# Another table of rank corrections and other tiling weights in the list scheduler of an attention kernel with a second, adapter attention

## The chip, the cores and the metric

The kernel runs on one NeuronCore of a Trainium2 chip. One execution of the whole program is timed on the device, in microseconds; the time of a version is the median of its runs. Engines are named as the profile names them: PE is TensorE, PEld its loading of weights, DVE VectorE, ACT ScalarE, POOL GpSimd and SP the engine that issues most of the transfers.

## The reference, cut to what matters

`x` is (2, 2048, 640), the context (2, 128, 384); there are 8 heads of 80. In what follows S is 2048, the last T = 4 rows of the context are `ca`, the 124 ahead of them `enc`.

```python
query  = x @ Wq                                   # (2, 2048, 640)
hs     = mha(query, enc @ Wk, enc @ Wv)           # text attention, 124 keys
ca_q1  = einsum('btc,th->bch', ca, Wq_ca)         # (2, 384, 640): one row for each of the 384 features of ca
ca_q1  = ca_q1[:, linspace(0, 383, S).astype(int)]  # row s of the output uses one of these 384 rows
ca_hs1 = mha(ca_q1, x, x)                         # the adapter's first attention, over all 2048 rows of x
ca_hs2 = mha(ca_hs1 @ Wq, ca @ Wk_ca, ca @ Wv_ca) # its second one, over 4 keys
out    = (hs + ca_hs2) @ Wout + b_out + x
```

`mha(q, k, v)` splits the 640 columns into 8 heads, and is softmax(q k^T / sqrt(80)) v for each head. All is float32.

## The kernel before, in words

**Tiles.** The 2 x 2048 rows of x are cut into 8 blocks of 512 rows, written (batch, number), and into 16 units `m` of 256 rows, two tiles of 128 each.

**Queries.** `queries_fast` multiplies a block by Wq in a scheme of four "chains" of products on sums of halves of x and Wq: matmuls `pq`, weights 128x128, 256 columns each, inputs `xt` (x transposed), `xs` (differences of x) and `wq_sb`. A product collected in a PSUM bank is copied to `q` by ACT or DVE if it is the first of its part, and added by DVE otherwise. The fifth group of 128 columns goes by `plain`; its result leaves for device memory through ACT and DVE (`halves_away`) and comes back in another layout over `landing`, by four transfers on SP (`rest_back`), from which ACT copies the `rests`.

**Text attention of a unit.** `text_scores`: matmuls `sc`, in tiles of 64x128, for each of the two row tiles. `softmax`: DVE's maximum `m`, eight exponentials `p` on ACT with their sums, a reciprocal `r`, the normalization (by whichever of POOL, DVE and ACT is free first), then DVE's transpose into `eb`, of which there is one buffer, and a transfer of `eb` to `kept` in device memory. `probabilities` brings `kept` back as `pT` (two buffers) and calls `text_out_fast`: matmuls `ph` in tiles of 128x32 into `hs` (copied by ACT or DVE), then matmuls `po` with Wout or sums of it, 128x128, 320 columns each, in four chains; DVE adds every result to the unit's rows of x. These rows lie in eight buffers (`x_more` and `last_rows`), are loaded by `residual` through SP and stored when complete. The adapter's result for those rows is added to them by a gathering transfer on POOL.

**Adapter, one pass for each batch.** `yz_block` makes for each block the operands `yz` and `zop` of x times the adapter's weights, and through DVE (`zs`, `yt`) and device memory the rows `y_sb`. The first loop of `adapter` runs over 4 blocks, 3 column tiles and 2 halves: four matmuls `s` (32x128) into a buffer of four PSUM banks, `quad`, then DVE's maximum `mx` of all four. There is one `quad`, so each piece of `s` waits for the maximum of the piece before. After the 24 maxima comes the **hand-over**: DVE writes `mt`, PE turns it (`pm`), DVE adds it to `ca`, ACT and DVE make the operand `cop` of it. Then the second loop, 24 pieces for each of two halves `j`: matmuls `s` into `quad`, ACT's exponential `ea`, and matmuls `acc` (128x32) with `y_sb` by `contract`. `second` does the attention over four keys with the result. The pass of batch 1 begins while that of batch 0 ends:

```python
        if b + 1 < B:
            yield Fork(adapter(b + 1), 0)
```

**What sets the order.** None of this is written in the order in which it runs. Each of the functions above is a generator that yields steps `Do(engine, fn, ...)`, and a class `Desk` replays them while the program is built, with estimated durations (`matmul`, `transpose`, `__getattr__`, `dma`). In `run` it takes at each point the engine that can begin something first, and among the steps that could begin at that earliest time on that engine the one with the least sum of two numbers:

```python
                    t, op = min(
                        (x for x in found if x[0] <= t + 1e-9),
                        key=lambda x: self.order(x[1]) + self.change(x[1].mode),
                    )
```

`order` is the rank that the code gives to the task or the step (for instance 10 + 2n for the queries of block n, 30 + m for the output of unit m, 2 + 0.1n for the loads of x of block n), plus a correction for this one task: `begin` counts the tasks of each name as they are begun and looks the n-th of them up in the table `RANKS`. A task is one run of a generator, so "chain" 30 is the 31st chain to be begun, of the queries' or of the output's, and "softmax" 21 the 22nd row tile. A lower number goes first. `change` is a weight that is added only where the step is marked with a tiling of PE (`mode`) other than the present one: `LEAVE` if the present one is the whole array (128x128), `SWITCH` for going back to the whole array, `ANOTHER` between two others. Only `pq`, `sc`, `ph` and `po` are marked.

The times and tilings serve only to choose. What is built is a fixed list of instructions for each engine, in the order in which the steps were taken (line 208 of the profile is the one place where matmuls are issued, 218 transposes, 233 everything of DVE, ACT and POOL, 253 SP's transfers, 2107 POOL's gathers), and waits on data and buffers hold them together on the chip. Where a step may go to several engines, the replay also decides which one does it.

Of the kernel before, what the change touches and what calls it, by code (L numbers as in the profile page):

```python
# [14 lines left out]
P = 128  # L15
# [49 lines left out]
class Desk:  # L65
# [1 line left out]


    ENGINES = ("PE", "ACT", "DVE", "POOL", "SP", "NONE")
    WHOLE, SWITCH, LEAVE, ANOTHER = (P, P), 157.7, 5.4, 131.2  # L70
    START = {(P, P): 0.107, (64, P): 0.143, (P, 64): 0.107, (64, 32): 0.1, (P, 32): 0.03}
    DRAIN = {
        ((P, P), (32, P)): 0.136, ((P, P), (64, P)): 0.035, ((P, P), (P, 64)): 0.056, ((P, P), (P, 32)): 0.067,
# [9 lines left out]


    RANKS = {
        "adapter": {0: 3, 1: 5.5},
        "chain": {2: 9, 4: -18, 5: 11, 6: -3, 8: -1, 10: -8, 11: -0.6, 19: -3, 24: -3, 25: 8, 30: 11, 32: 8,
            34: -10, 35: -1, 36: -1.3, 39: 2, 41: 3.5, 42: 4, 45: 6, 48: -4, 49: -15, 52: -1, 53: 6, 58: 8,
            60: -6, 61: -6, 62: -9, 64: -1, 72: -3, 80: 2, 85: 3, 87: 7},
        "contract": {0: 5.5, 1: 6, 2: 6, 3: 8},  # L90
        "halves_away": {1: -13, 2: -2, 6: 7},
        "keys": {0: -11},
        "probabilities": {0: 6.1, 8: 9, 9: 6, 11: -7, 14: -3, 15: 4},
        "queries_fast": {0: 4, 4: -3},
        "rest_back": {1: 13, 4: 5, 9: 7, 10: 8},
        "second": {0: 6},
        "softmax": {0: 6, 2: -2, 4: -5, 8: 5, 10: 4, 11: -4, 14: -4, 16: 2, 17: 7, 21: 12, 22: 10, 25: 4},
        "sums_of_wq": {0: 9},
        "text_scores": {0: -3, 1: 9, 12: 5},
        "values_weights": {0: -17},  # L100
        "x_load": {1: 5.1, 4: 7, 5: 6},
        "y_rows": {2: 4, 3: 15, 5: -2},
        "yz_block": {2: 12, 3: -2, 6: 10, 7: 1.3},
    }

    def __init__(self, tc):
# [2265 lines left out]
```

## Time and profile before

| | |
|---|---|
| median of 3 runs | 588.07 us (587.85 to 589.9) |
| profiled execution, its own time | 588.11 us |
| its span in the trace | 586.4 us |
| granted clock of PE | full in all 40 slices |
| PE | 578.6 us busy, 99%, 4681 instructions |
| weight loads, PEld | 374.8 us, 64% |
| DVE | 392.0 us, 67% |
| ACT | 313.2 us, 53% |
| POOL | 141.7 us, 24% |
| moved by transfers | 112.27 MB, mean 191 GB/s |

The span is the time between the first and the last record of the trace; the execution's own time has something more around it. "Busy" for PE counts a matmul from its start to a modelled end, and matmuls overlap in the pipeline, so that PE's share hides short waits. DVE, ACT and POOL are counted by records with measured ends. A line of groups gives line, engine, operation, output and inputs with shapes, the count, then the busy time and the mean of one in ns, then the idle time ahead and what ended most of it. A line of the chain or of the timeline begins with the start and the duration in us. A line of waits names who waited, for whom, and the total, the count and the longest.

### The profile page before, as it was taken

Reading aid. Unit: us, or ns where it says so; the run is one execution under the profiler, and the core shown is the slowest. Engines: PE = TensorE matmul, PEld = TensorE weight load, DVE = VectorE, ACT = ScalarE, POOL = GpSimd, SP = SyncE. Lnnn points to the kernel's source line nnn. Section 1 sums busy time; section 2 is a strip of 40 time slices with the busy share of each in tenths; the row PEclk is TensorE's granted clock in tenths of the full one; section 3 lists DMA queues with packets and bytes.
Section 4 is the critical chain, followed back from the end, with each engine's and each line's share of the span. In section 5 each row is a group of like instructions: output and inputs, shape, how many; then the busy total and the mean of one; then the engine's idle time right before and its main releaser. Section 6 shows DMA issues by size and latency. Waiting matters only on the chain.

```text
span 586.4 us, 12250 instructions
## 1 busy us (share of the span) xinstructions
PE 578.6 (99%) x4681; PEld 374.8 (64%) x4681; DVE 392.0 (67%) x646; ACT 313.2 (53%) x881; POOL 141.7 (24%) x200
## 2 busy tenths in 40 slices
PE   9999999999999999999999999999999999999997
PEld 8786446676766566566576656655556566676675
DVE  2546899999999566356999999853255353544443
ACT  1413276686558789679847626368678612102200
POOL 9102112112205214010115225122041221322342
PEclk9999999999999999999999999999999999999999
DMA  8996876899566967324999959994658577699967
GB/s 254 231 215 116 204 105 180 173 212 182 148 198 149 219 144 193 114 75 155 246 264 260 235 150 206 295 265 122 154 124 248 128 198 201 142 261 267 264 162 195
DMA packets 153012, 112.27 MB, mean 191 GB/s; under 512 B 83701, under 2 KB 126581, under 8 KB 152954
## 3 DMA queue, kind: packets, MB, share of 16 engines
q1 hardware_dynamic: 147322, 100.80, 66.5%
q0 software_dynamic: 5632, 10.69, 10.5%
q8 instruction: 37, 0.61, 0.4%
q14 instruction: 21, 0.17, 0.1%
HBM read 71.23 MB, written 40.22 MB: 190 GB/s over the span
## 4 chain that ended last, share of the span: by engine, by line
PE 85%; DVE 9%; DMA 2%; issue 2%; ACT 2%; DVEq 0%
PE po L208 27%; PE pq L208 23%; PE acc L208 7%; PE ph L208 7%; PE sc L208 6%; PE s L208 6%; DVE mx L233 4%; PE pyz L208 2%; DVE eb L233 1%; PE pv L208 1%; PE pk L208 1%; DMA kept<-eb 1%; DMA zb<-z 1%; DVE m L233 1%; PE unread L208 1%
## 5 line engine op out<-in xcount | busy, mean ns | idle before, releaser
L233 DVE TENSOR_REDUCE mx<-s 128x4 f32<-128x2048 f32 x48 | 109.3, 2276 | 2.4 <-PE s L208 2.4
L233 ACT ACTIVATE ea<-s 128x2048 f32<-128x2048 f32 x48 | 91.0, 1895 | 30.8 <-PE s L208 30.6
L233 ACT ACTIVATE p<-sc,m 128x124 f32<-128x124 f32 x256 | 89.8, 383 | 7.5 <-DVE m L233 6.8
L208 PE MATMUL pq<-xt,wq_sb 128*128 128x256 f32 (+1 forms) x312 | 86.2, 416 | 0.1
L208 PE MATMUL po<-wout_sums,hs 128*128 128x320 f32 x256 | 78.9, 440 | 0.5 <-DVE x_more L233 0.5
L208 PE MATMUL po<-wout_sb,hs 128*128 128x320 f32 x248 | 76.6, 439 | 0.0
L233 DVE TENSOR_TENSOR x_more<-x_more,po 128x320 f32<-128x320 f32 x76 | 36.5, 484 | 52.3 <-PE po L208 51.8
L208 PEld LDWEIGHTS pq<-xt,wq_sb 128*128 128x128 f32 x312 | 56.8, 190 | 21.3 <-issue 13.7
L208 PEld LDWEIGHTS po<-wout_sums,hs 128*128 128x128 f32 x256 | 47.2, 190 | 23.6 <-issue 4.7
L208 PEld LDWEIGHTS po<-wout_sb,hs 128*128 128x128 f32 x248 | 45.6, 190 | 22.8 <-issue 4.2
L233 ACT ACTIVATION_READ_ACCUMULATOR p<-sc,m 128x1 f32 x256 | 57.9, 226 | 0.0
L2107 POOL DMA_INDIRECT x_more<-o,query x19 | 29.4, 1550 | 101.2 <-DVE x_more L233 86.5
L208 PE MATMUL acc<-ea,y_sb 128*32 128x384 f32 (+2 forms) x768 | 51.2, 385 | 0.0
L233 DVE TENSOR_REDUCE m<-sc 128x4 f32<-128x496 f32 x64 | 40.0, 662 | 11.2 <-PE sc L208 11.1
L233 DVE TENSOR_TENSOR last_rows<-last_rows,po 128x320 f32<-128x320 f32 x52 | 25.0, 485 | 31.6 <-PE po L208 31.2
L233 ACT COPY hs<-ph 128x512 f32<-128x512 f32 (+1 forms) x34 | 18.3, 545 | 51.7 <-PE ph L208 51.7
L208 PE MATMUL ph<-pT,vpad 128*32 128x256 f32 x768 | 45.0, 381 | 0.0
L233 ACT ACTIVATE p<-p,r 128x124 f32<-128x124 f32 x120 | 36.3, 387 | 10.9 <-DVE r L233 10.9
L233 POOL TENSOR_TENSOR p<-p,r 128x992 f32<-128x992 f32 x8 | 14.8, 1853 | 112.8 <-DVE r L233 112.8
L233 DVE STREAM_TRANSPOSE eb<-p 128x1024 f32<-128x1024 f32 x32 | 39.4, 1232 | 1.9 <-DMA kept<-eb 1.1
L208 PE MATMUL pq<-xt,wq 128*128 128x512 f32 (+1 forms) x90 | 40.1, 564 | 0.0
L208 PEld LDWEIGHTS sc<-kmain,q 64*128 64x128 f32 x512 | 31.5, 187 | 11.4 <-issue 6.1
(212 smaller groups left out, 814.7 us busy)
## 6 DMA issues: line engine op xcount, KB each, us to landing
kept<-eb SPq DMA_DIRECT2D x32, 512.0 KB, 4.4
pT<-kept SPq DMA_DIRECT2D x64, 256.0 KB, 6.7
landing<-away SPq DMA_DIRECT2D x60, 128.0 KB, 3.6
xi<-in_x_dram SPq DMA_DIRECT2D x56, 128.0 KB, 3.9
x_more<-in_x_dram SPq DMA_DIRECT2D x19, 320.0 KB, 6.6
out_dram<-x_more SPq DMA_DIRECT2D x18, 320.0 KB, 4.9
last_rows<-in_x_dram SPq DMA_DIRECT2D x13, 320.0 KB, 5.5
y<-yt SPq DMA_DIRECT2D x16, 256.0 KB, 3.5
```

Source lines behind the costliest of these rows:

```text
L208: self.pin(self.nc.tensor.matmul(out, lhsT, rhs, **kw))
L233: self.pin(getattr(engine, what)(*args, **kw))
L2107: desk.pin(nc.gpsimd.indirect_dma_start(out=t, out_offset=None, in_=o2_of[b], in_offset=bass.IndirectOffsetOnAxis(ap=query[:, st : st + 1] ...
```

## The change

Two things in `Desk` are replaced, and nothing else. The three weights of `change` become larger: 328.5 for 157.7 (`SWITCH`), 9.9 for 5.4 (`LEAVE`) and 185.7 for 131.2 (`ANOTHER`). And `RANKS`, the table of corrections for single tasks, is another one: tasks named in it go earlier or later in the replay than before. Every function that yields steps, every shape, buffer and estimated duration stays, and so do the numbers of matmuls and transfers; what differs in the program is the order of instructions on each engine, and for a few steps that more than one engine may do, the engine. The whole diff:

```diff
--- before.py
+++ after.py
@@ -67,7 +67,7 @@
 
 
     ENGINES = ("PE", "ACT", "DVE", "POOL", "SP", "NONE")
-    WHOLE, SWITCH, LEAVE, ANOTHER = (P, P), 157.7, 5.4, 131.2
+    WHOLE, SWITCH, LEAVE, ANOTHER = (P, P), 328.5, 9.9, 185.7
     START = {(P, P): 0.107, (64, P): 0.143, (P, 64): 0.107, (64, 32): 0.1, (P, 32): 0.03}
     DRAIN = {
         ((P, P), (32, P)): 0.136, ((P, P), (64, P)): 0.035, ((P, P), (P, 64)): 0.056, ((P, P), (P, 32)): 0.067,
@@ -83,24 +83,25 @@
 
 
     RANKS = {
-        "adapter": {0: 3, 1: 5.5},
-        "chain": {2: 9, 4: -18, 5: 11, 6: -3, 8: -1, 10: -8, 11: -0.6, 19: -3, 24: -3, 25: 8, 30: 11, 32: 8,
-            34: -10, 35: -1, 36: -1.3, 39: 2, 41: 3.5, 42: 4, 45: 6, 48: -4, 49: -15, 52: -1, 53: 6, 58: 8,
-            60: -6, 61: -6, 62: -9, 64: -1, 72: -3, 80: 2, 85: 3, 87: 7},
-        "contract": {0: 5.5, 1: 6, 2: 6, 3: 8},
-        "halves_away": {1: -13, 2: -2, 6: 7},
-        "keys": {0: -11},
-        "probabilities": {0: 6.1, 8: 9, 9: 6, 11: -7, 14: -3, 15: 4},
-        "queries_fast": {0: 4, 4: -3},
-        "rest_back": {1: 13, 4: 5, 9: 7, 10: 8},
-        "second": {0: 6},
-        "softmax": {0: 6, 2: -2, 4: -5, 8: 5, 10: 4, 11: -4, 14: -4, 16: 2, 17: 7, 21: 12, 22: 10, 25: 4},
-        "sums_of_wq": {0: 9},
-        "text_scores": {0: -3, 1: 9, 12: 5},
-        "values_weights": {0: -17},
-        "x_load": {1: 5.1, 4: 7, 5: 6},
-        "y_rows": {2: 4, 3: 15, 5: -2},
-        "yz_block": {2: 12, 3: -2, 6: 10, 7: 1.3},
+        "adapter": {0: 1, 1: 2},
+        "chain": {2: 8, 4: -11, 5: 7, 6: -2, 8: -11, 11: -4, 14: 11, 15: 16, 19: -14, 24: -4, 25: 3, 30: 3.1,
+            32: 4, 34: 10, 36: 2, 41: 0.5, 42: 1, 43: 0.5, 44: -10, 45: -10, 48: -8, 50: -5, 51: -5, 52: 7,
+            54: 10, 55: 10, 56: 10, 68: -4, 76: -3, 81: 2, 86: 2, 87: 3},
+        "contract": {0: 5, 1: 4.5, 2: 8, 3: 8},
+        "halves_away": {1: -4, 2: -2, 4: 4, 6: 6},
+        "keys": {0: -10},
+        "probabilities": {3: -8, 5: -4, 8: 12, 9: -3, 10: -2, 12: 6, 13: 6, 15: 7},
+        "queries_fast": {0: 5, 3: 4},
+        "rest_back": {1: 11, 4: 5, 7: 8, 9: 9, 10: 5, 14: 2},
+        "second": {0: 2.3},
+        "softmax": {0: 5, 2: -7, 3: 6.2, 4: -4, 7: -11, 8: 2, 10: -5, 12: -20, 14: -3, 17: 9, 20: -2, 21: 7,
+            22: 7, 25: -5, 29: 2, 30: 6},
+        "sums_of_wq": {0: 5.7},
+        "text_scores": {0: -8, 1: 3.4, 12: 9},
+        "values_weights": {0: -18},
+        "x_load": {1: 4.2, 4: 5},
+        "y_rows": {2: 2, 3: 6, 4: 4},
+        "yz_block": {2: 16, 5: 3.5, 6: 5},
     }
 
     def __init__(self, tc):
```

## Prediction

> **What bounds the kernel now.** I read the page first, then TensorE's waits, then the chain of work that ended last, then pieces of the timeline.
>
> ```profile
> span 586.4 us, 12250 instructions
> ...
> PE 578.6 (99%) x4681; PEld 374.8 (64%) x4681; DVE 392.0 (67%) x646; ACT 313.2 (53%) x881; POOL 141.7 (24%) x200
> ...
> DVE  2546899999999566356999999853255353544443
> ...
> PEclk9999999999999999999999999999999999999999
> ```
>
> TensorE (PE) works from end to end at full clock; VectorE (DVE) is full only in slices 6 to 13 and 20 to 25 of 14.66 us, about 73 to 190 and 279 to 366 us. The profiled execution took 588.11 us, 1.7 around its span, beside a median of 588.07: I sum against the former and carry the difference over unchanged.
>
> ```profile
> PE pm L218 <- ACT p L233: 0.7, 1, 0.7
> PE s L208 <- DVE mx L233: 0.6, 1, 0.6
> PE po L208 <- DVE x_more L233: 0.5, 1, 0.5
> ```
>
> These are the longest of TensorE's waits in the answer for 170 to 400 us (waiter, releaser; total, count, longest, us), and they look like nothing. But modelled ends hide short ones, so I compared starts with what the steps should take. The chain gives the steps:
>
> ```profile
> 1.12 3.78 PE unread L208 x16
> ...
> 7.19 8.65 PE pq L208 x40
> ...
> 197.95 1.86 PE acc L208 x32
> ...
> 203.24 1.00 PE acc L208 x16
> ...
> 553.47 29.28 PE po L208 x108
> ```
>
> A 256-column row steps by 8.65 / 40 = 0.216 us, a 320-column row by 29.28 / 108 = 0.271. A change of tiling costs something on top:
>
> ```profile
> 227.93 1.07 PE L208 MATMUL acc<-ea,y_sb 128*32 128x384 f32 x16
> 228.93 2.86 PE L208 MATMUL pq<-xt,wq_sb 128*128 128x256 f32 x12
> 231.72 0.56 PE L208 MATMUL s<-cop,zop 32*128 32x128 f32 x8
> ```
>
> From the start of pq to that of s are 2.79 us, and 12 rows are 2.59: leaving the whole array costs 0.20. Two acc pieces take 1.86, one 1.00, so a piece is 0.86 and leaving 128x32 costs 0.14. Summing columns and changes so over all 4681 rows from the first start (1.12), TensorE would end at 572.3 us; it ends at 553.47 + 29.28 = 582.7, after which the last addition and store take 3.7. So 10.3 us are lost in waits: by the starts, 3.5 before 105 us (the cold stretch and the first loads), 1.5 from 105 to 187, 0.8 to 265, 2.2 to 310, 0.4 to 363, 0.8 to 392 and 1.1 from there to the end. That list is all a new order has to win from, except for the changes of tiling themselves.
>
> **The change, part by part.** Only order moves: both programs hold the same 2803 matmuls, 441 transfers on SP and 64 on POOL. So I read the built orders.
>
> *Tiling weights.* 157.7 or 328.5 for going back to the whole array, 131.2 or 185.7 for going to a third tiling: each exceeds every difference of rank there is, so "stay in the tiling if anything is ready" holds before and after. Counted in the orders, stretches of one tiling go from 303 to 301: whole array 103 to 100, 128x32 63 to 64, the other kinds unchanged. That is 3 x 0.20 - 0.14 = 0.46 us less. [...]
>
> *Same order, same waits.* TensorE's order is the old one up to 152 us (but for one piece of pq at 105) and again from 252 to 310. The 3.5 and the 2.2 us stay; in the latter DVE is full with the maxima and its order is the old one but for which half of zop comes when.
>
> *First hand-over, 152 to 187 us.* The matmuls of the s loop wait for DVE's maximum of the piece before.
>
> ```profile
> L233 DVE TENSOR_REDUCE mx<-s 128x4 f32<-128x2048 f32 x48 | 109.3, 2276 | 2.4 <-PE s L208 2.4
> L233 ACT ACTIVATE ea<-s 128x2048 f32<-128x2048 f32 x48 | 91.0, 1895 | 30.8 <-PE s L208 30.6
> ...
> L233 DVE STREAM_TRANSPOSE eb<-p 128x1024 f32<-128x1024 f32 x32 | 39.4, 1232 | 1.9 <-DMA kept<-eb 1.1
> ```
>
> I step through DVE's new order by the trace's durations (less 0.08 each, by which DVE's rows overlap), from a maximum that stands where it stood:
>
> ```profile
> 155.85 2.28 DVE L233 TENSOR_REDUCE mx<-s 128x4 f32<-128x2048 f32 x1
> ...
> 173.62 2.28 DVE L233 TENSOR_REDUCE mx<-s 128x4 f32<-128x2048 f32 x1
> ```
>
> It ends at 158.1. An addition to q, one eb, a reciprocal and, newly ahead, three xt take 3.6: next maximum 161.7 to 164.0, and TensorE asks at 164.9. Then zs, q, yt and two m, 3.0: maximum 166.9 to 169.2, asked for at 168.9, so 0.3 us of waiting. Then zs, a reciprocal and eb: maximum 171.0 to 173.3, in time. Then q, yt, xt and two m: the last maximum ends at 178.6, and behind another eb mt comes at 180.5, 0.1 late for pm. TensorE's next pq want the banks that the two additions to mt free, 0.25 and 0.2 late, as an xt, two q, a difference of x and an m are queued ahead of them. Before, pm had to wait 0.7 us for a bank that ACT's exponentials held; now more pq stands ahead of pm, and that goes. With what is lost from 137 to 155 us as before, 1.3 replaces 1.5.
>
> *ACT's loop, 187 to 265 and from 385 on.* Each s2 waits for the exponential ea of the piece before, 1.9 us. Comparing, from each ea to the next, ACT's work with TensorE's, the places where ACT has more sum to 16.2 us before and 11.4 after; most are caught up from slack. I take 0.2 us off each of the two stretches.
>
> *Second hand-over, 363 to 392 us.* Before, it runs like this:
>
> ```profile
> 370.88 0.50 PE L208 MATMUL s<-zop,cop 32*128 32x512 f32 x4
> 376.46 0.52 PE L218 MATMUL pm<-ident,mt 128*128 128x128 f32 x3
> 378.40 0.55 PE L218 MATMUL pm<-ident,mt 128*128 128x128 f32 x3
> 385.57 0.50 PE L208 MATMUL s<-cop,zop 32*128 32x384 f32 x8
> ```
>
> ```profile
> 382.27 6.33 DMA kept<-eb
> 388.69 1.25 DVE eb L233
> 390.36 1.34 PE po L208 x4
> ```
>
> ```profile
> 379.67 0.55 DVE L233 TENSOR_TENSOR mt<-ca,pm 128x384 f32<-128x384 f32 x1
> ...
> 383.31 1.01 DVE L233 SCALAR_TENSOR_TENSOR cop<-cop,low_c,mt 128x768 fp32r<-128x768 f32 x1
> ```
>
> From the last s of one pass to the first of the next are 14.7 us; in between DVE takes the maximum, mt, two additions and cop. Shortly after, an eb waits 6.33 us for the store of the one before (there is one buffer), DVE's queue stands, and po waits 0.57 for an addition behind it. In the new order only 12.0 us of TensorE's work lie between the two s, but DVE's share there is shorter: 0.5 to the maximum's start, 2.2 for it, 1.2 for one eb, three additions, mt and pm 0.4 + 0.9, two additions to mt 0.55 each with others between, ACT's copy of cop some 0.9, cop 1.0. Queued in that order cop is done 10.1 us after the s, 1.9 before TensorE asks. The wait of eb for its store comes again (two stand 5 us of DVE work apart), but at a place where TensorE next asks DVE some 3 us later. So 0.7 of the 0.8 us go; if that cover is gone, they stay.
>
> *Softmax shares.* Two normalizations go from ACT (8 instructions each) to DVE, and two change between DVE and POOL. All of DVE's additional ones lie past 205 us and outside its full slices. Nothing.
>
> *Loads, on SP's queue.* The transfers of xi for block (1,2) now go ahead of the four of landing for scores 14, which are needed some 6 us after they would be in. In TensorE's steps, a buffer of pT is free at least 19 us before its next unit is multiplied (15 before), and a buffer of rows has 28 us between its users (30 before); gathers on POOL keep their number and follow the units. The first load of a second half of zop, moved behind others, is asked for some 6 us after its place in the queue. I cost all this at nothing: that slack hides it, and past it each microsecond of lateness is one of TensorE's.
>
> Sum: 0.46 + 0.2 + 0.2 + 0.7 + 0.2, and 0.1 from the stretch at 310 to 363, where the last maxima stand 1.4 us wider apart: 1.9 us. 588.1 - 1.9 = 586.2.
>
> **The rivals.** *The waits only move* (588.11 - 0.46 = 587.6). For it: waits of TensorE answered through DVE or ACT that fall short by durations alone number 7 in either order, 0.7 us together; under 0.2 us of slack are 17 before, 16 after. The orders are equally tight, and what one gives another takes. 20%.
>
> *Nearly all goes* (583.7): of what isn't shared, 1.5 + 0.8 + 0.4 + 0.8 + 1.1 = 4.6 us, 4.0 vanish, with the 0.46. For it: ACT's shortfalls shrink, DVE's maxima from 323 to 363 us get more room. Against: my stepping finds 1.3 us of fresh waits in the first hand-over alone. 24%.
>
> *DVE's queue is late in both hand-overs* (591.4, slower). From the maximum at 155.85 to that at 173.62 the new order gives DVE 2.7 us more work for 1.5 us more of TensorE's. If DVE paces all of it, TensorE loses 1.2; if the second chain is again 14.7 us long in place of 12.0, 2.7. 588.1 - 0.5 + 1.2 + 2.7 = 591.5, less 0.1 for the wider maxima. It decides from where cop is ready more than 12 us after the last s. Against: in the old chain 5 us are additions, m and a second eb that now stand elsewhere. 10%.
>
> **How the numbers follow.** The forecast has 46%, on its own 585.2 to 587.2. An edge of 0.5% (2.9 us, about what a measurement of this kernel can tell from no change) lies at 585.1 and 591.0. Faster: the second rival and a rim of the forecast, 25%. Slower: the third, 10%. Within: 65%. The range goes down to 583.6, to hold the second rival, and up to 590.0, over the first and over half of what the third could cost.
>
> **What would show it.** Right: 301 stretches, TensorE's last row some 1.9 us earlier, the wait of pm for ACT p gone, po's wait for x_more near 390 gone, s from 265 to 310 waiting as before. Wrong: a new wait over 1 us of s2 for cop after 376, of sc for rests near 209, or of s for mx before 175; or TensorE's loss from 187 on below 3 us, which would make the second rival true.

## The result: 0.2% faster, where 0.3% was forecast

Over 20 runs each the changed kernel takes 587.84 us (586.80 to 590.36) and the kernel before 588.79 (587.85 to 590.88). The medians lie 0.95 us apart; the ratio of the two groups is 0.998, 95% interval 0.9971 to 0.999, which is 1.2 us less (0.6 to 1.7). A later group of runs gave 587.25 (12 runs) and 588.52, ratio 0.9982 (0.9974 to 0.9991). The forecast was 1.9 us less; the sign was right, the size was not.

The profiled execution of the changed kernel took 587.70 us. The page of after, the parts that answer to those of before (span, busy time, the slices of VectorE, the granted clock):

```profile
span 586.0 us, 12235 instructions
...
PE 578.5 (99%) x4681; PEld 374.4 (64%) x4681; DVE 394.2 (67%) x648; ACT 308.2 (53%) x865; POOL 141.0 (24%) x200
...
DVE  2546899999999756256999999874455253444343
...
PEclk9999999999999999999999999999999999999999
```

Nothing here shows where the time went: TensorE is busy as before; VectorE is 2.2 us busier, as it does 11 of the normalizations in place of 9, and ScalarE does two fewer. TensorE's waits from 170 to 400 us in after (waiter, releaser; total, count, longest):

```profile
PE s L209 <- DVE mx L234: 1.0, 2, 0.6
PE pq L209 <- DVE mt L234: 0.6, 1, 0.6
PE sc L209 <- ACT p L234: 0.3, 1, 0.3
```

Two of the three rows of before are gone, pm for ACT p and po for x_more; in their place stand a wait of pq for mt and one of sc for ACT p. TensorE's last piece in the chain that ended last is this:

```profile
562.76 19.59 PE po L209 x72
```

TensorE's last row of work thus ends at 562.76 + 19.59 = 582.35 us, 0.4 earlier than before. The sum without waits, by the steps and changes of the prediction, ends at 571.85 for the new order and 572.28 for the old. So the first trace of after says: 0.44 us won by changes of tiling, and lost in waits 10.33 us in place of 10.29. (Lost time is taken at the starts of rows; between the ends it comes out 0.2 us larger in both.)

That would have been the rival "the waits only move", to the tenth (587.6 forecast, 587.70 measured). It is not what the times say, and more traces show why. Lost time by stretch, the starts of TensorE's rows less the sum without waits, in us; the last column is the time of the execution that left the trace:

| trace | to 40 | 40-152 | 152-187 | 187-265 | 265-310 | 310-363 | 363-392 | to end | all | time |
|---|---|---|---|---|---|---|---|---|---|---|
| before | 3.73 | 0.22 | 1.15 | 0.48 | 2.47 | 0.47 | 0.52 | 1.25 | 10.29 | 588.11 |
| before, second | 3.47 | 0.21 | 0.80 | 0.91 | 2.40 | 1.41 | 1.27 | 1.44 | 11.92 | 589.76 |
| before, third | 2.84 | 0.16 | 1.02 | 0.71 | 2.79 | 0.72 | 0.67 | 1.50 | 10.42 | 588.24 |
| after | 3.21 | 0.23 | 1.44 | 0.66 | 2.72 | 1.15 | -0.14 | 1.06 | 10.33 | 587.70 |
| after, second | 3.12 | 0.14 | 1.51 | 0.69 | 2.37 | 0.84 | -0.21 | 1.13 | 9.59 | 586.97 |
| after, third | 3.32 | 0.22 | 1.45 | 0.68 | 2.39 | 1.35 | -0.15 | 1.07 | 10.34 | 587.72 |
| mean after less mean before | -0.13 | 0.00 | +0.48 | -0.02 | -0.06 | +0.24 | -0.99 | -0.31 | -0.79 | |

With the 0.44 of the sum without waits, the means differ by 1.23 us, as the times do. The negative numbers, down to -0.21, show how far the sum itself is off in a stretch; why was not looked into. With three traces of each kernel, a difference can be put down to the order where the three of one kernel lie apart from the three of the other: from 152 to 187, from 363 to 392, and to the end. In the other stretches the traces of the two kernels overlap. The first trace of before was of a quick execution (588.11 beside a median of 588.79): its loss in waits was the smallest of three.

### The profile page after: what moved, and what is told of

It is laid out like the page before. It is cut to its first block, busy times and chain, and to the rows that moved or that the text cites. A ratio compares the mean times of both kernels' runs of the same rounds, so it can differ in the third digit from the quotient of the medians.

```text
span 586.0 us, 12235 instructions
## 1 busy us (share of the span) xinstructions
PE 578.5 (99%) x4681; PEld 374.4 (64%) x4681; DVE 394.2 (67%) x648; ACT 308.2 (53%) x865; POOL 141.0 (24%) x200
## 4 chain that ended last, share of the span: by engine, by line
PE 81%; DVE 7%; DMA 5%; ACT 3%; issue 1%; SPq 1%; DVEq 0%; ACTq 0%
PE po L209 27%; PE pq L209 21%; PE acc L209 7%; PE ph L209 7%; PE s L209 6%; PE sc L209 5%; DVE mx L234 3%; PE pyz L209 2%; DMA x_more<-in_x_dram 2%; ACT p L234 1%; SPq L254 1%; ACT ea L234 1%; PE pv L209 1%; PE pk L209 1%; DMA zb<-z 1%
## 5 line engine op out<-in xcount | busy, mean ns | idle before, releaser
L209 PE MATMUL po<-wout_sb,hs 128*128 128x320 f32 x240 | 74.6, 439 | 0.1
L234 DVE TENSOR_TENSOR x_more<-x_more,po 128x320 f32<-128x320 f32 x72 | 34.5, 483 | 48.0 <-PE po L209 47.6
L2108 POOL DMA_INDIRECT x_more<-o,query x18 | 27.9, 1550 | 126.0 <-DVE x_more L234 91.5
L209 PEld LDWEIGHTS po<-wout_sb,hs 128*128 128x128 f32 x240 | 44.2, 190 | 21.9 <-issue 2.5
L234 DVE TENSOR_TENSOR last_rows<-last_rows,po 128x320 f32<-128x320 f32 x56 | 26.8, 482 | 29.0 <-PE po L209 27.3
L234 POOL TENSOR_TENSOR p<-p,r 128x992 f32<-128x992 f32 x8 | 14.7, 1843 | 127.0 <-DVE r L234 127.0
L209 PE MATMUL sc<-kmain,q 64*128 64x124 f32 x512 | 38.3, 285 | 0.3 <-ACT p L234 0.3
```

Source lines behind the costliest of these rows:

```text
L209: self.pin(self.nc.tensor.matmul(out, lhsT, rhs, **kw))
L234: self.pin(getattr(engine, what)(*args, **kw))
L2108: desk.pin(nc.gpsimd.indirect_dma_start(out=t, out_offset=None, in_=o2_of[b], in_offset=bass.IndirectOffsetOnAxis(ap=query[:, st : st + 1] ...
```

## Experiments: the weight and the table, apart

With SWITCH and ANOTHER alone at their new values, every engine's list is that of before: of the three weights only LEAVE acts. Three kernels take it and the table apart:

```diff
 e1_leave (before, and)
-    WHOLE, SWITCH, LEAVE, ANOTHER = (P, P), 157.7, 5.4, 131.2
+    WHOLE, SWITCH, LEAVE, ANOTHER = (P, P), 157.7, 9.9, 131.2
 e2_ranks (after, and)
-    WHOLE, SWITCH, LEAVE, ANOTHER = (P, P), 328.5, 9.9, 185.7
+    WHOLE, SWITCH, LEAVE, ANOTHER = (P, P), 157.7, 5.4, 131.2
 e7_no_table (after, and)
-    RANKS = { ... }
+    RANKS = {}
```

> The kernel before, its table of ranks kept, with the weight LEAVE at 9.9 in place of 5.4 (the other two weights, put to the new values alone, leave every engine's order as it was). The built order has 314 stretches of one tiling on TensorE in place of 303, and TensorE's sum without waits ends at 574.3 us in place of 572.3. Theory 'TensorE's sum decides, waits only move': lost time stays near 10.3 us in the trace, and the kernel is slower than before by 2.0 us (ratio 1.0035). Rival 'changes of tiling hide in waits': within 0.5 us of before. Rival 'table and weight were fitted to each other': waits grow too, slower by 4 us or more (ratio over 1.007).

> The new table of ranks with the three old weights. 311 stretches of one tiling, TensorE's sum without waits ends at 573.7 us, 1.4 later than before and 1.9 later than after the change. Theory 'TensorE's sum decides, waits only move': lost time 10.3 us in the trace, 1.4 us slower than before (ratio 1.0024). Rival 'hidden': within 0.5 us of before. Rival 'fitted to each other': slower than before by 3.5 us or more.

> The changed kernel with an empty table of ranks (weights 328.5, 9.9 and 185.7). 313 stretches of one tiling, TensorE's sum without waits ends at 574.1 us. Theory 'a table is worth what it was fitted for, and with another weight it is worth nothing': as slow as the two mixed kernels, 606 to 616 us. Rival 'a foreign table does harm': clearly faster than those, 592 to 602 us.

Measured: the weight alone 613.25 us (ratio 1.0432, 1.0412 to 1.0451), the table alone 614.25 (1.0433, 1.0416 to 1.0449), no table 608.83 (1.0357, 1.0315 to 1.0399). For the first two the direction is that of "fitted to each other", but the size, 25 and 26 us, none of the theories had. The kernel without a table, asked for after these two, lies in the range of its own theory (606 to 616) and not in that of the rival (592 to 602). Still, with the new weights the old table is somewhat worse than no table, by the intervals of 6 and 4 runs; the old weights without a table were not run. The traces lost 26.6 us (in an execution of 606.65 us, the quickest of its six), 35.4 and 29.9 us. In both mixed kernels the order leaves the one it was fitted for early (at 83 and 103 us of the replay). What the corrections then do to tasks that stand among other neighbours was not followed one by one.

Most of the loss is waits. By its page TensorE is busy for 585.6 us of a span of 604.9 in e1_leave, and for 578.6 of 586.4 in before: of the 18.5 us that this execution took longer, 11.5 are idle time of TensorE, and 2.0 are changes of tiling by the sum. Another part is not waits but a slower clock. In the timeline of e1_leave, a wait of 2.77 us is followed by a piece that takes 3.31 us:

```profile
188.28 3.31 PE L208 MATMUL pyz<-xt,wyz 64*32 64x512 f32 x32 [2.77 <-DVE xt L233]
```

The window on that stretch (from and to; its length; busy time and number of instructions of PE, PEld, DVE, ACT and POOL; TensorE's granted clock; the DMA share and GB/s):

```profile
189.00:191.00 2.00, 2.00 (x32) 0.45 (x16) 2.00 (x2) 2.00 (x11) 1.31 (x2) 0.50 0.88 243
```

From 189 to 191 us the granted clock is 0.50. The same in e2_ranks (0.50 from 160 to 164 us), after the 4.07 us for a maximum:

```profile
158.54 0.51 PE L209 MATMUL s<-zop,cop 32*128 32x512 f32 x4 [4.07 <-DVE mx L234]
160.70 3.78 PE L209 MATMUL pq<-xt,wq_sb 128*128 128x256 f32 x8 [1.66 <-ACT p L234]
```

Eight rows of pq take 3.78 us there, and 1.89 at full clock (182.61 in after, below). How large this part is, the mean granted clock of each run bounds: 0.985 to 0.994 in e1_leave and 0.989 to 0.992 in e2_ranks, so at most 0.6% to 1.5% of the span, 4 to 9 us of their 25. Without a table two of the four runs had a granted clock of 1.000 and took 607.08 and 607.51 us, 19 us more than before.

## Experiments: one half of the order each

TensorE's list has the same set of rows behind it in both orders at 270 us of the replay. Two kernels have the order of all engines written out, step by step, in place of the choice by rank:

```diff
     def run(self):
-        while any(self.queue.values()): ...   # the earliest engine, its lowest rank
+        for engine, step in TAKEN: ...        # e3: before's steps to 270 us, then after's; e4 the reverse
```

> The order of before up to 270 us of the replay, from there the order of after: each engine's list is written out, the steps are the same. TensorE's sum without waits ends at 571.99 us (302 stretches). From the two traces: before loses 2.4 us between 20 and 265 us, after 4.1 to 4.4 from 280 on. Theory 'waits only move': lost time 9.9 to 10.3 us, and the time is 0.3 to 0.6 us under before; the waits of pm for ACT p near 180 (0.7) come as before, the long wait of pq for mt near 185 (0.6) does not, po's wait for an addition near 390 does not. Rival 'the gain is in the first half': equal to before within 0.2 us. In the time itself the theories differ by less than one run's scatter; the losses by stretch in the trace decide.

> The order of after up to 270 us of the replay, from there the order of before. TensorE's sum without waits ends at 572.14 us (302 stretches). Theory 'waits only move': lost time 10.3 to 10.6 us; the wait of pq for mt near 185 us (0.6) is there, the hand-over at 376 to 392 loses 0.5 us again, and sc near 310 loses 0.2 and not 0.6; the time is 0.1 under to 0.3 us over before. Rival 'the gain is in the first half': 1.0 us under before.

| trace | to 40 | 40-152 | 152-187 | 187-265 | 265-310 | 310-363 | 363-392 | to end | all |
|---|---|---|---|---|---|---|---|---|---|
| e3, before then after | 3.76 | 0.14 | 1.14 | 0.48 | 2.47 | 1.06 | -0.15 | 1.07 | 9.98 |
| e4, after then before | 3.73 | 0.20 | 1.49 | 0.68 | 2.37 | 0.30 | 1.45 | 1.00 | 11.23 |

From 152 to 310 us the stretches repeat what their order lost in one of its own traces, to 0.05 us: 1.14 and 1.49 to 187, 0.48 and 0.68 to 265. From 363 to 392 the new order again loses nothing (-0.15); the old one loses 1.45, where its own three traces have 0.52 to 1.27. So the gain at the second hand-over and the loss at the first belong to the parts of the order in which they stand. 310 to 363 did not carry over, and neither did the last stretch: with the old order it lost 1.00 us in e4, as little as with the new one. The times cannot decide: e3 587.50 beside 588.06 of before (0.9993, 0.9984 to 1.0001), e4 588.44 (1.000, 0.9991 to 1.0009); neither is told from before by its interval. The rival that the gain lies in the first half wanted e4 1.0 us under before; by the ratio it came out level, by the medians 0.4 over.

## Experiments: more traces of the same kernels

> The changed kernel once more, unaltered, for a second trace and times beside those of before on one chip. Its first trace lost 0.5 us less than before's up to 40 us, where both orders are the same; in the two hybrids that stretch lost 3.73 and 3.76 us, as in before (3.73). Theory 'the start is chance, the rest belongs to the order': up to 40 us 3.2 to 3.8, and from 40 us on each stretch as in the first trace within 0.1 us, 7.1 us in all against 6.6 of before; so after's gain is 0.46 - 0.5 = about nothing in a typical execution and the ratio comes out at 0.999 to 1.001. Rival 'the first trace was an unlucky one': the waits at 185 (pq for mt, 0.6) and 310 (sc for ACT p, 0.3) are smaller or gone, and the ratio is near 0.998 again.

> The kernel before, for a second trace. Its first trace was of an execution of 588.11 us, under the medians of the three groups of its runs (588.79, 588.06 and 588.52). Theory 'a chance wait': sc waits for ACT p near 310 us, as in two of three traces with the same order there, because the zb that was copied to zop lands later; then 7.2 to 7.4 us are lost from 40 us on in place of 6.56. Rival 'always the same': 6.5 to 6.7.

> The kernel before, a third trace: the same two theories, 7.2 to 7.4 us lost from 40 us on, or 6.5 to 6.7.

> The changed kernel, a third trace: from 40 us on 7.1 us lost (with the wait of sc for ACT p near 310 us) or 6.5 (without).

From 40 us on before lost 6.56, 8.45 and 7.58 us, after 7.11, 6.48 and 7.02. So "the rest belongs to the order" is wrong for the stretch from 310 to 363 in both kernels, and for 363 to 392 in before. The wait of pq for mt near 185 us, 0.6, came in all three traces of after, against the rival that it was bad luck. What varies from 310 to 363 hangs on when a cast on ScalarE can start, and it waits for a transfer. The timeline of before's first trace, ScalarE's cast of zop and TensorE's sc behind it (in brackets the wait and its releaser):

```profile
308.19 0.62 ACT L233 CAST zop<-zb 128x512 fp32r<-128x512 f32 x1 [1.38 <-DMA zb<-z]
...
310.39 1.15 PE L208 MATMUL sc<-kmain,q 64*128 64x124 f32 x14
```

and of its second:

```profile
308.86 0.62 ACT L233 CAST zop<-zb 128x512 fp32r<-128x512 f32 x1 [1.62 <-DMA zb<-z]
...
310.93 1.25 PE L208 MATMUL sc<-kmain,q 64*128 64x124 f32 x14 [0.72 <-ACT p L233]
```

and after's third:

```profile
308.76 0.62 ACT L234 CAST zop<-zb 128x512 fp32r<-128x512 f32 x1 [2.08 <-DMA zb<-z]
...
310.82 1.25 PE L209 MATMUL sc<-kmain,q 64*128 64x124 f32 x14 [0.50 <-ACT p L234]
```

The cast waits for zb, and ScalarE's exponentials p, which free the bank that sc needs, stand behind the cast. What counts is where the cast stands against TensorE. Measured from the start of the same row of pq (304.78 us in before's first trace), it starts 3.4 and 3.6 us later in before's first and after's second trace, and sc waits for nothing; it starts 3.9 to 4.3 us later in the other four, and sc waits 0.3 to 0.7 us, longer the later the cast. That is up to three quarters of a microsecond by chance in either order, and the two traces first compared had drawn differently.

From 363 to 392 it is the old order's hand-over that varies. TensorE's timeline of before's second trace:

```profile
371.88 0.50 PE L208 MATMUL s<-zop,cop 32*128 32x512 f32 x4
382.76 2.80 PE L208 MATMUL ph<-pT,vpad 128*32 128x256 f32 x48
386.76 0.51 PE L208 MATMUL s<-cop,zop 32*128 32x384 f32 x8
391.63 0.54 PE L208 MATMUL po<-wout_sums,hs 128*128 128x320 f32 x1 [0.57 <-DVE x_more L233]
```

Again 14.9 us from the last s to the first of the next pass (14.7 in the first trace), the wait of po for an addition again, and 1.27 us lost in place of 0.52. Why the same order lost more than twice as much there was not found.

## Experiments: the first hand-over, queue place by queue place

A queue place is where a step stands in the list of its engine. In the three traces of before, and in those of after, TensorE, VectorE, ScalarE and GpSimd each work their list off in one and the same order, so that a step comes after all that stand ahead of it.

In after, TensorE at the first hand-over:

```profile
182.22 0.55 PE L219 MATMUL pm<-ident,mt 128*128 128x128 f32 x3
182.61 1.89 PE L209 MATMUL pq<-xt,wq_sb 128*128 128x256 f32 x8
185.09 1.99 PE L209 MATMUL pq<-xt,wq_sb 128*128 128x256 f32 x8 [0.59 <-DVE mt L234]
186.92 1.89 PE L209 MATMUL pq<-x_sums,wq_sums 128*128 128x256 f32 x8
```

and VectorE:

```profile
181.80 0.54 DVE L234 TENSOR_TENSOR mt<-ca,pm 128x384 f32<-128x384 f32 x1
182.27 1.72 DVE L234 TENSOR_TENSOR x_sums<-xt 128x512 f32<-128x512 f32 x1
183.91 0.66 DVE L234 TENSOR_REDUCE m<-sc 128x4 f32<-128x496 f32 x1
184.50 0.54 DVE L234 TENSOR_TENSOR mt<-ca,pm 128x384 f32<-128x384 f32 x1
```

pq at 185.09 wants the bank that the second addition to mt frees. This addition stands behind a difference of x and one maximum m, and ends at 185.04. One step was moved:

```diff
 VectorE, e6_mt_first
   x_sums<-xt (difference of x)
-  m<-sc
   mt<-ca,pm (second)
+  m<-sc
```

> The order of after with one step moved: on VectorE the second addition to mt (184.50 in after's trace) goes ahead of one maximum m of the scores (183.91); every other engine's list is the same. Theory 'TensorE's 0.6 us at 185 is this one queue place': pq's wait for mt falls from 0.59 to 0.1 or less, the loss from 175 to 187 us from 1.2 to 0.6, the later stretches stay, and span and time are 0.5 us shorter than after's. Rival 'the wait moves on': the loss by 230 us is the same as in after, since sc or s2 wait for the exponentials that start 0.5 us later behind m.

The wait for mt went, and the next pq waited. TensorE, then ScalarE, in e6_mt_first:

```profile
182.40 3.91 PE L432 MATMUL pq<-xt,wq_sb 128*128 128x256 f32 x16
187.09 1.97 PE L432 MATMUL pq<-x_sums,wq_sums 128*128 128x256 f32 x8 [0.78 <-ACT q L457]
```

```profile
184.94 0.36 ACT L457 ACTIVATE p<-sc,m 128x124 f32<-128x124 f32 x1 [2.19 <-DVE m L457]
...
185.63 0.83 ACT L457 CAST cop<-mt 128x768 fp32r<-128x768 f32 x1
186.35 0.59 ACT L457 COPY q<-pq 128x512 f32<-128x512 f32 x1
```

The exponentials p start when m is done, and m now stands behind the addition; cop and the copy of q stand behind them, and the third pq waits 0.78 us for that copy. The stretches 152 to 187 and 187 to 265 lost 0.88 + 1.60 in place of 1.44 + 0.66: the wait had moved on, and more. The median is 588.38 us, ratio 0.9996 to before (0.9986 to 1.0005), where after had 0.9982 in the same group of runs. The rival was right in this.

The next kernel moves the copy of q too, and three other steps:

```diff
 e9_five_places (the order of after, with)
 VectorE:  mt (second) ahead of m, as in e6
 VectorE:  mx (at 288) ahead of the step that begins the attention over four keys
 ScalarE:  q<-pq ahead of p<-sc,m (at 184.5)
 ScalarE:  accs<-acc ahead of the last two p<-sc,m (at 280)
 ScalarE:  zop<-zb behind four p<-sc,m (at 308)
```

> The order of after with five queue places changed, nothing else: on VectorE the second addition to mt ahead of one m (as in the run before) and one maximum mx ahead of the step that begins the attention over four keys (near 286 us); on ScalarE one copy of q ahead of the exponentials that stood before it (near 184.5), the copy of accs ahead of the last two exponentials (near 280), and the cast of zop behind four exponentials (near 308). Theory 'each wait is one queue place': pq's waits near 185 and 187 us both go (0.6), pt_acc's 0.4, the wait of s for mx near 290 (0.6), sc's wait for ACT p near 310 where it comes (0.7 in two of three traces with that order): from 40 us on 5.0 to 5.3 us are lost in place of 6.5 to 7.1, and time and span are 1.5 us under after's, 2.5 under before's (ratio 0.9957). Rival 'waits only move': at least 6.3 us are lost from 40 us on, ratio 0.998 as after's.

TensorE's waits from 170 to 400 us, and its timeline at the first hand-over:

```profile
PE pt_p L442 <- DVE p2pad L457: 0.5, 1, 0.5
PE pq L432 <- ACT p L457: 0.2, 1, 0.2
PE s L432 <- ACT ea L457: 0.2, 1, 0.2
```

```profile
182.99 3.90 PE L432 MATMUL pq<-xt,wq_sb 128*128 128x256 f32 x16
186.73 1.89 PE L432 MATMUL pq<-x_sums,wq_sums 128*128 128x256 f32 x8
```

The three pieces of pq now follow without a gap, from the last pm to the next s. From 40 us on 5.67 us are lost (after: 6.48 to 7.11), less than the rival's 6.3 and more than the 5.0 to 5.3 of the theory. Of the five places, that of mx did not pay: the wait of s went, and pt_p now waits 0.5 us for p2pad, whose step mx has overtaken. The time is 586.76 us beside 588.79 of before, ratio 0.9968 (0.9955 to 0.9981), where after had 0.998 and 0.9982. That it beats before is shown. That it beats after is not: the intervals overlap, the two were not run in one group, and e9 left one trace.

One attempt at a better mixture failed: before's steps to 323.5 us of the replay, after's from there, and one cast on ScalarE moved.

> The order of before up to 323.5 us of the replay and that of after from there (TensorE's sum without waits 571.99 us, 302 stretches), and on ScalarE one cast of wq_sums (177.38 in before) behind the exponentials that free the bank for which pm waits. Theory 'each stretch keeps the loss of its order': lost time 9.98 us of the first hybrid, less 0.5 to 0.8 between 310 and 325 us (sc for ACT p, which only after's order had) and less 0.35 for pm: 8.9 to 9.2, a span 1.0 to 1.3 us under before's. Rival 'waits only move': lost time stays at 10 us, span 0.3 us under before's.

It took 597.28 us (1.0142, 1.0124 to 1.016). ScalarE's moved cast did its part (0.86 us lost from 152 to 187), but at the seam pT came late. TensorE in e8_best_of_both:

```profile
321.49 3.16 PE L432 MATMUL ph<-pT,vpad 128*32 128x256 f32 x32 [3.04 <-DVE m L457]
334.29 5.15 PE L432 MATMUL ph<-pT,vpad 128*32 128x256 f32 x48 [4.55 <-DMA pT<-kept]
```

Before's 48 rows of ph took 2.80 us (382.76, above), these take 5.15. The windows give the reason, the granted clock (the third number from the end):

```profile
314.00:318.00 4.00, 4.00 (x34) 2.74 (x33) 4.00 (x4) 2.87 (x13) 2.05 (x2) 1.00 1.01 203
321.40:323.00 1.60, 1.51 (x20) 1.04 (x24) 0.07 (x1) 0.02 (x1) 0.00 (x0) 0.70 1.07 399
323.00:325.00 2.00, 2.00 (x20) 0.84 (x12) 0.00 (x0) 0.88 (x2) 0.73 (x1) 0.50 1.09 284
325.00:327.00 2.00, 2.00 (x23) 0.93 (x20) 1.57 (x1) 2.00 (x11) 1.49 (x3) 0.89 0.09 19
336.00:339.00 3.00, 3.00 (x35) 1.53 (x28) 0.00 (x0) 1.17 (x2) 1.07 (x2) 0.50 0.00 0
```

Why pT was late at the seam was not settled. TensorE's lists had the same rows behind them there, but the other engines' lists differed.

## Why the prediction was right in sign and wrong in size

The working has 1.9 us less, the means of the traces 1.23. One term accounts for the gap, the first hand-over; what the others missed, both ways, nearly cancels, which is luck. Of the signs that it named, 301 stretches came and both waits went (pm for ACT p, po for x_more), and s waited as before but for 0.4 us more in one trace. TensorE's last row was not 1.9 us earlier but 0.4 in the first pair of traces.

*Changes of tiling, 0.46 us:* the sum by steps gives 0.44, and the means of the traces add up to the measured time with it; no run isolates it. The reason given for it was incomplete: the prediction weighed SWITCH and ANOTHER, which change nothing, and passed over LEAVE, a number of the size of the ranks, which alone changes the order from 83 us of the replay on (e1_leave).

*First hand-over, 0.2 us won:* this is the step that failed, the stepping through VectorE's queue that replaced 1.5 us of lost time by 1.3. The stretch from 152 to 187 lost 1.44 to 1.51 us in after and 0.80 to 1.15 in before: 0.5 more in the mean, where 0.2 less was forecast. The prediction named the right queue, "an xt, two q, a difference of x and an m" ahead of the additions to mt, and put the two late by 0.25 and 0.2; the second alone held pq for 0.6. It also took before's loss from one trace, the highest of three.

*ACT's loop, 0.2 us twice:* from 187 to 265 nothing was won (0.70 and 0.68 in the mean): the forecast gain from fewer places where ScalarE has more work than TensorE did not come. To the end 0.31 was won, but e4 lost as little there with the old order, so that this gain is not shown to be the order's.

*Second hand-over, 0.7 us:* right in the mechanism, step by step. TensorE and VectorE in after:

```profile
373.24 0.51 PE L209 MATMUL s<-zop,cop 32*128 32x512 f32 x4
379.16 0.49 PE L219 MATMUL pm<-ident,mt 128*128 128x128 f32 x3
380.03 0.49 PE L219 MATMUL pm<-ident,mt 128*128 128x128 f32 x3
385.30 0.51 PE L209 MATMUL s<-cop,zop 32*128 32x384 f32 x8
```

```profile
373.80 2.29 DVE L234 TENSOR_REDUCE mx<-s 128x4 f32<-128x2048 f32 x1
...
382.08 1.02 DVE L234 SCALAR_TENSOR_TENSOR cop<-cop,low_c,mt 128x768 fp32r<-128x768 f32 x1
```

From s at 373.24 to s at 385.30 are 12.06 us (12.0 forecast), and cop is done at 383.10, 9.9 us after the s (10.1 forecast), so nothing waits. The gain is 0.66 us against the first trace of before and 0.99 against the mean, as the old order lost 0.52, 0.67 and 1.27 there. (The working had put 0.8 in this stretch and 0.8 in that from 187 to 265 of the first trace, where the table has 0.52 and 0.48.) The rival with VectorE late in both hand-overs is refuted by these rows.

*310 to 363 us, 0.1 won:* 0.24 lost in the mean, but the traces of the two kernels overlap (0.47 to 1.41 and 0.84 to 1.35), and up to 0.7 us of it hangs on when the cast of zb starts. The prediction did not have this wait: it put the loads that are moved at nothing, and this one isn't moved.

*265 to 310 the same:* 2.55 and 2.49 in the mean. Right.

Term by term, with the means: -0.44 +0.48 -0.02 -0.06 +0.24 -0.99 -0.31, and -0.13 by the start, which is the same order in both: -1.23. The rival "the waits only move" had the first pair of traces for it. The times are against it: its 0.46 us lies outside both intervals, 0.6 to 1.7 us and 0.5 to 1.5.

## What to carry to other kernels

A kernel whose engine waits for many small things loses by queue places, and each can be named: find the step that frees the bank, see what stands ahead of it on its engine, and see who waits for that before moving it, as e6 did not. Ranks that a search has found belong to the weights they were found with: here either without the other cost twenty times what the two together brought. Before a difference of 1 us is explained from traces, take three of each kernel: here one execution's waits differ by up to 1.6 us from the next one's.

## What was not expected of the hardware

A wait of TensorE can cost more than itself. In e8_best_of_both the granted clock fell to half from about 322 us, after a wait of 3.04 us, and by the windows up to 327 us (0.70, 0.50 and 0.89) TensorE was at half clock for 1.0 + 2.0 + 0.4 = 3.4 us; after 4.55 us it was at half clock again (0.50 from 336 to 339 us), and 48 rows took 2.35 us longer. In no trace of before, after or e9 is there a wait over 1.1 us, and the granted clock is 0.999 or 1.000. But a single wait of 3 us is not needed. The longest wait in the trace of e7_no_table is 1.6 us, and its mean granted clock is 0.991 over 608.4 us, by an estimate from these two numbers about 11 us at half clock, if nothing but half and full clock was granted. Two of its windows and a piece of its timeline:

```profile
113.20:116.60 3.40, 2.41 (x30) 1.84 (x28) 3.40 (x4) 1.74 (x11) 0.00 (x0) 1.00 0.88 203
116.60:120.00 3.40, 3.40 (x11) 2.42 (x12) 3.40 (x6) 1.97 (x12) 1.29 (x1) 0.50 1.04 203
```

```profile
117.10 3.42 PE L190 MATMUL pq<-x_sums,wq_sb 128*128 128x256 f32 x8
```

TensorE was idle for 1.0 us of the 3.4 ahead, and eight rows of pq then took 3.42 us in place of 1.89. In e1_leave, 1.43 us of waiting in a row (at 194.51) was followed by no half clock (1.00 from 193 to 197). So the length of the wait alone does not decide; what else does stays open.
